# Three elementwise steps of an attention and expert layer put on ScalarE instead of VectorE

## The chip, the core and the metric

The kernel runs on one core of one Trainium2 chip. The metric is the device time of the whole kernel in microseconds, the median over several executions. Five engines work side by side, each through its own queue in order: TensorE (PE in the profile, PEld for its weight loads), VectorE (DVE), ScalarE (ACT), GpSimd (POOL) and SyncE (SP), which issues the transfers.

## The reference

A layer over 8 rows of 512 tokens with 256 features. Each row is normalised, and goes into an attention and a feed-forward part, whose outputs are added to the input.

The attention has 16 heads of 16 features and three branches: attention to 32 compressed blocks of 16 tokens, attention to the tokens of four chosen blocks, and attention to the last 32 tokens. The blocks are chosen by the compressed logits:

```python
logits_c = jnp.where(c_ok, s_b, NEG)
out_c = jnp.einsum('bhtn,bhnd->bhtd', jax.nn.softmax(logits_c, axis=-1), v_c)
_, top_idx = jax.lax.top_k(logits_c, r_eff)            # r_eff = 4
tok = (top_idx[..., None] * G + jnp.arange(G)).reshape(B, H, T, r_eff * G)
```

Three gates from a softmax weigh the branches. The feed-forward part is a gated network with 1024 hidden units, plus a retrieval of experts: for each of 4 heads the top 8 of 64 keys on two axes are taken, the best 8 of the 64 sums of pairs are kept, and each kept pair names one of 1024 experts, weighted by a softmax:

```python
sc, ix = jax.lax.top_k(sim, KPH)                       # KPH = 8
all_ix = (ixx[..., :, None] * NKEYS + ixy[..., None, :]).reshape(b, t, H, KPH * KPH)
scores, pk = jax.lax.top_k(all_sc, KPH)
```

## The kernel before

The work is cut into 8 rows, 32 tiles of 128 tokens (four to a row) and 16 halves of 256 tokens. Each stage is a Python generator that is run over all rows, tiles or halves. Weights stay in SBUF, but for the gated network's first weights, which are loaded again for each half (`fetch`).

**What sets the order.** No order is written by hand. The class `Conductor` (lines 164 to 251) plans: each stage yields the engine and the buffers or events it needs next; the planner takes, among the stages that could start within 0.12 us of the earliest, the one with the lowest rank (the numbers of the `each` lines, 1184 to 1202), lets it issue until its next yield, and books the instructions. Its costs are a fixed part and a part for each element (lines 169 to 171, and a hop from engine to engine). Lines 204 to 210 book that GpSimd and VectorE exclude each other, on VectorE's side only for `tensor_tensor` and `scalar_tensor_tensor` without an operand in PSUM. So the queue of each engine is a result of these costs, and any edit of a stage can change the order of all queues. All instructions go through one helper, so they all have line 160 in the profile's compiled copy; they are told apart by the tiles they write and read.

**The stages that matter here.**
- `layernorm` (479): per row, mean and variance of four tiles (bn_stats, bn_aggr), the square root on ACT, a reciprocal with one correction step, then for each tile `xn` = (x - mean) x rs on DVE (507), two transposes on PE, and a copy to `xnT` by ACT. There is one `xn` buffer.
- `queries` (670): projections and the compressed logits `lg`, with a low value where a block is not allowed.
- `logits` (701): q times k of all tokens up to the tile's end into PSUM; DVE takes block maxima `bm` and window maxima `ml`.
- `select` (758): per head the eight largest compressed logits; the first four are replaced by BIG in a copy `mr` (match_replace, 779); line 783 turns the copy into marks, 0 for a chosen block and -1e30 otherwise; the marks are added to `bm`, the maximum `ms` is taken, and GpSimd writes marks minus `ms` into the extended query `ext`, which PE transposes. `mr` has one buffer.
- `weights` (862) and `products` (913): PE multiplies the extended queries with the keys into pairs of PSUM banks, ACT writes the exponential `wT`, PE multiplies it with the values. There are two pairs, and a step takes both.
- `choose_experts` (977): per tile and head, max and index of the top 8 (`top`, `ixu`), two subtractions into `ed`, the cast of the indices to bf16 `ix` (997), two comparisons with a table (`at_y`, which lies in a `big` buffer, and `at_x`), sums of pairs, their top 8, counts, and the exponentials `et` and `ed` on ACT.
- `route` (1054): four times per tile a comparison into `big` on DVE and several 128x1024 products and sums (`big`, `gw`) on GpSimd.
- `experts`, `hidden`, `project` (1083, 1123, 1165): the large products; ACT and DVE finish `aT`, `xg` and `hT`.

Of the kernel before, what the change touches and what calls it, by code (L numbers as in the profile page):

```python
# [11 lines left out]
AF = mybir.ActivationFunctionType  # L12
ALU = mybir.AluOpType
# [3 lines left out]
P = 128  # L17
# [5 lines left out]
NT = T // P  # L23
# [11 lines left out]
OUT = -1.0e30  # L35
BIG = 3.0e38
HALF_BIG = 1.0e38

_CONST_COLS = [
    ("ident", P), ("any", 1), ("grp", 4), ("head4", H),  # L40
# [59 lines left out]
def bc(ap, axis, n):  # L100
    a = ap.unsqueeze(axis)
    shape = list(a.shape)
    shape[axis] = n
    return a.to_broadcast(shape)
# [150 lines left out]
def tile_kernel(ctx, tc, x, wq, wk, wqT, wv, wo, wck, wcv, wga, bga, wgu, bg, bu, wd, bd,  # L255
# [5 lines left out]
    pe, vec, act, pool, sp = (Engine(con, e, n) for e, n in (  # L261
        (nc.tensor, "PE"), (nc.vector, "DVE"), (nc.scalar, "ACT"), (nc.gpsimd, "POOL"),
        (nc.sync, "SP")))
# [4 lines left out]
    def buf(name, shape, dt=F32):  # L268
        return cp.tile(shape, dt, name=name, tag=name)

    def stock(name, n, shape, dt=F32):
        return Stock(con, [buf(f"{name}{i}", shape, dt) for i in range(n)])
# [18 lines left out]
    def load_x(b, t):  # L291
        sp.dma_start(out=t, in_=x[b].rearrange("(i p) d -> p i d", p=P))
# [55 lines left out]
    bd_s = weight("bd_s", bd.partition_broadcast(P), [P, DM])  # L348
    eps_s = buf("eps_s", [P, 1])
    vec.memset(eps_s, EPS)  # L350
    bgh = buf("bgh", [P, 8])
    vec.tensor_scalar(bgh, bg_s, 0.5, None, ALU.mult)

# [30 lines left out]
    xn1 = stock("xn", 1, [P, DM])  # L384
# [7 lines left out]
    mrs = stock("mr", 1, [P, H, 4 + NB])  # L392
# [8 lines left out]
    top, ixu = buf("top", [P, 2 * PH, KPH]), buf("ixu", [P, 2 * PH, KPH], U32)  # L401
    ix = buf("ix", [P, KPH, 2 * PH], BF16)
# [35 lines left out]
    PE, DVE, ACT, POOL, SP = "PE", "DVE", "ACT", "POOL", "SP"  # L438
# [28 lines left out]
    def to_heads(src, dst):  # L467

        def to_pe(pt):
            for g in range(4):  # L470
                pe.transpose(heads4(pt.ap)[:, g, :], src[:, g].rearrange("p j n -> p (j n)"), ident)
        def to_sb(pt):
            act.copy(dst, heads4(pt.ap))
            pt.free()
        return to_pe, to_sb
# [3 lines left out]
    def layernorm(s):  # L479

        if s.b == 0:
            xl = first_x
            yield DVE,
        else:
            xl = yield SP, xls
            load_x(s.b, xl.ap)
            yield DVE,
        mv, st = buf_mv, buf_st
        for i in range(NT):
            vec.bn_stats(out=st, in_=xl.ap[:, i, :])  # L490
            vec.bn_aggr(out=mv[:, i, :], in_=st)
            yield DVE,
        vec.tensor_scalar(buf_ve, mv[:, :, 1], EPS, None, ALU.add)
        yield ACT,
        act.activation(buf_rs, mv[:, :, 1], AF.Sqrt, bias=eps_s)
        yield DVE,
        rs, cor = buf_rs, buf_cor
        vec.reciprocal(rs, rs)

        vec.tensor_tensor(cor, rs, rs, ALU.mult)  # L500
        vec.tensor_tensor(cor, cor, buf_ve, ALU.mult)
        vec.tensor_scalar(cor, cor, -0.5, 1.5, ALU.mult, ALU.add)
        vec.tensor_tensor(rs, rs, cor, ALU.mult)
        s.xnT = yield None, xnTs
        for i in range(NT):
            xn = yield DVE, xn1
            vec.tensor_scalar(xn.ap, xl.ap[:, i, :], mv[:, i, 0:1], rs[:, i:i + 1],
                              ALU.subtract, ALU.mult)
            pt = yield PE, banks
            p2 = pt.ap[:, :DM].rearrange("p (c n) -> p c n", c=2)  # L510
            for c in range(2):
                pe.transpose(p2[:, c, :], xn.ap[:, c * P:(c + 1) * P], ident)
            xn.free()
            yield ACT,
            act.copy(s.xnT.ap[:, :, i * P:(i + 1) * P], p2)
            pt.free()
        xl.free()
        s.done("xn")

    buf_mv, buf_st = buf("mv", [P, NT, 2]), buf("st", [P, 6])  # L520
    buf_ve, buf_rs, buf_cor = buf("ve", [P, NT]), buf("rs", [P, NT]), buf("cor", [P, NT])

    def prepare_keys(s):
# [234 lines left out]
    def select(t):  # L758

        s, i = t.row, t.i  # L760
        nb = (i + 1) * (P // G)
        yield None, t.ev("lg")
        lg = t.lg.ap
        mr, t.ec = yield None, mrs, ecs
        for h in range(H):
            if h % 4 == 0:
                yield DVE,
            vec.max(out=t8[:, h, :], in_=lg[:, h, 4:4 + nb])
        yield POOL,
        pool.tensor_copy(mx, t8[:, :, 0])  # L770
        pool.tensor_tensor(t.ec.ap, lg[:, :, 4:], bc(mx, 2, NB), ALU.subtract)
        t.done("ec")
        yield DVE,

        vec.memset(t8[:, :, R:], BIG)
        for h in range(H):
            if h % 4 == 0:
                yield DVE,
            vec.match_replace(out=mr.ap[:, h, :4 + nb], in_to_replace=t8[:, h, :],
                              in_values=lg[:, h, :4 + nb], imm_value=BIG)  # L780
        t.lg.free()
        sel = mr.ap[:, :, 4:]
        vec.tensor_scalar(sel[:, :, :nb], sel[:, :, :nb], HALF_BIG, OUT, ALU.is_lt, ALU.mult)
        yield DVE, t.ev("s")
        bmf = t.bm.ap.rearrange("p g j n -> p (g j) n")
        vec.tensor_tensor(bmf[:, :, :nb], bmf[:, :, :nb], sel[:, :, :nb], ALU.add)
        vec.tensor_reduce(ms, bmf[:, :, :nb], AX.X, ALU.max)
        t.bm.free()
        t.qx = {}
        for v in ((2, 0) if i < 2 else (2, 0, 1)):  # L790
            e, t.qx[v] = yield POOL, exts, qxs
            ef = e.ap.rearrange("p g j n -> p (g j) n")
            pool.tensor_copy(ef[:, :, :D], t.q.ap.rearrange("p g j n -> p (g j) n")[:, :, :D])
            if v == 2:
                pool.tensor_scalar(ef[:, :, G:], bc(t.ml.ap.rearrange("p g j -> p (g j)"), 2, G),
                                   -1.0, None, ALU.mult)
                t.ml.free()
            else:
                w = min(G, nb - G * v)
                pool.tensor_tensor(ef[:, :, G:G + w], sel[:, :, v * G:v * G + w], bc(ms, 2, w),  # L800
                                   ALU.subtract)
            pt = yield PE, banks
            to_pe, to_sb = to_heads(e.ap, t.qx[v].ap)
            to_pe(pt)
            e.free()
            yield ACT,
            to_sb(pt)
            t.done(("qx", v))
        mr.free()
        t.q.free()  # L810
# [166 lines left out]
    def choose_experts(t):  # L977

        i = t.i
# [14 lines left out]
        vec.tensor_tensor(ed[:, :, :NK], sim[:, PH:, :], bc(top[:, PH:, 0], 2, NK), ALU.subtract)  # L994
        vec.tensor_tensor(ed[:, :, NK:], sim[:, :PH, :NX], bc(top[:, :PH, 0], 2, NX), ALU.subtract)
        pt.free()
        vec.tensor_copy(ix.rearrange("p j h -> p h j"), ixu)

        ayh = yield DVE, bigs
        at_y = ayh.ap.bitcast(BF16).rearrange("p (j y h) -> p j y h", y=NK, j=KPH)  # L1000
# [12 lines left out]
        yield DVE,  # L1013
        vec.tensor_scalar(pick, pick, HALF_BIG, None, ALU.is_gt)
        with nc.allow_low_precision(reason="counts up to 8"):
# [149 lines left out]
    def project(t):  # L1165
# [16 lines left out]
        t.yo.free()  # L1182

    each(rows, lambda s: 4 * s.b - 3.0, layernorm)
    each(rows, lambda s: 4 * s.b - 2.5, prepare_keys)
    each(rows, lambda s: 4 * s.b - 0.5, prepare_values)
    each(rows, lambda s: 99, release_row)
    each(tiles, lambda t: t.n, queries)
    each(tiles, lambda t: t.n + 0.1, logits)
    each(tiles, lambda t: t.n + 0.2, select)  # L1190
    each(tiles, lambda t: t.n + 0.3, compressed)
    each(tiles, lambda t: t.n + 0.3, weights)
    each(tiles, lambda t: t.n + 0.25, products)
    for jp in range(2):
        each(tiles, lambda t: t.n + 0.24, finish(jp))
    each(tiles, lambda t: t.n + 0.15, choose_experts)
    each(tiles, lambda t: t.n + 0.2, route)
    each(tiles, lambda t: t.n + 0.5, experts)
# [53 lines left out]
```

## Time and profile before

| | |
|---|---|
| Median of three runs | 1812.65 us (1808.81 to 1814.56) |
| Profiled execution | 1813.57 us, span 1811.8 us, granted clock 0.97 |
| VectorE instructions | 5292 |
| ScalarE instructions | 1370, among them 15 table loads (19.2 us) |
| GpSimd: 128x1024 products and sums, big | 224, 486.1 us, mean 2170 ns |
| GpSimd: 128x1024 products and sums, gw | 96, 228.1 us, mean 2376 ns |
| ScalarE: exponentials wT | 224, 217.6 us, mean 1021 ns |

The profile is one execution. "Busy" is the time in which an engine has an instruction running. The groups give a mean duration; the view of one tile gives the smallest, median and largest. The waits name the engine and the tile that a waiting instruction needed last. The chain of work that ended last is followed back from the last instruction, at each step to what released it or to the instruction before it on its engine.

### The profile page before, as it was taken

The numbers are of one execution on the slowest core, as the hardware profiler recorded it, in microseconds if no ns is written. First come the engines' busy times: TensorE is split into PE (matmuls) and PEld (weight loads), VectorE is DVE, ScalarE is ACT, GpSimd is POOL, SyncE is SP. The second block draws the span as 40 slices with busy tenths as digits, with TensorE's granted clock in tenths as the row PEclk, the third lists the DMA queues.
The fourth block names the chain that finished last, engine by engine and source line by source line (L and its number), as shares of the span: only waits on it lengthen the run. The fifth ranks groups of instructions, "written<-read, shape, count | busy, mean of one in ns | idle before, by whom it ended". The sixth has DMA issues, their size and how long they took to land.

```text
span 1811.8 us, 47633 instructions
## 1 busy us (share of the span) xinstructions
PE 1622.0 (90%) x19208; PEld 1246.5 (69%) x19208; DVE 1478.4 (82%) x5292; ACT 686.5 (38%) x1370; POOL 1012.4 (56%) x789
## 2 busy tenths in 40 slices
PE   3889879899899998999989998989979999898969
PEld 2667757777677766767667676766757777676757
DVE  2598799886977889898898967788897897979892
ACT  1344323444335243352343533344324434433233
POOL 2066546646475365665476754656647456575644
PEclk9999989999999999999999998999989999998989
DMA  5001001111001100001011110101001010100001
GB/s 181 10 21 37 19 19 31 31 40 24 24 25 37 37 26 25 24 26 38 16 34 31 32 31 20 36 26 37 25 18 31 15 40 28 31 19 24 25 11 32
DMA packets 55069, 56.12 MB, mean 31 GB/s; under 512 B 21696, under 2 KB 38080, under 8 KB 54848
## 3 DMA queue, kind: packets, MB, share of 16 engines
q1 hardware_dynamic: 54848, 53.07, 9.8%
q8 instruction: 151, 2.47, 0.6%
q14 instruction: 70, 0.57, 0.1%
HBM read 48.02 MB, written 4.19 MB: 29 GB/s over the span
## 4 chain that ended last, share of the span: by engine, by line
PE 55%; DVE 36%; ACT 3%; issue 3%; POOL 1%; DMA 1%; SPq 0%; DVEq 0%; ACTq 0%; POOLq 0%
PE psum L160 55%; DVE bm L160 6%; DVE big L160 4%; DVE pick L160 3%; DVE ixu L160 2%; DVE ml L160 2%; DVE mr L160 2%; DVE aT L160 2%; ACT wT L160 2%; DVE junk L160 2%; DVE hT L160 1%; DVE sums L160 1%; DVE top L160 1%; DVE at_x L160 1%; DVE xg L160 1%
## 5 line engine op out<-in xcount | busy, mean ns | idle before, releaser
L160 POOL TENSOR_TENSOR big<-big,ed 128x1024 f32<-128x1024 f32 x224 | 486.1, 2170 | 411.9 <-DVE big L160 359.2
L160 ACT ACTIVATE wT<-psum 128x1024 f32<-128x1024 f32 x224 | 217.6, 1021 | 167.6 <-PE psum L160 167.6
L160 PE MATMUL psum<-xnT,wb 128*128 128x256 f32 x1024 | 255.2, 393 | 9.1 <-DVE hT L160 5.6
L160 POOL TENSOR_TENSOR gw<-gw,big 128x1024 f32<-128x1024 f32 x96 | 228.1, 2376 | 7.0
L160 DVE TENSOR_REDUCE bm<-psum 128x32 f32<-128x512 f32 (+2 forms) x224 | 199.1, 911 | 32.3 <-PE psum L160 32.1
L160 PEld LDWEIGHTS psum<-xnT,wb 128*128 128x128 f32 x1024 | 191.7, 196 | 46.7 <-DVE hT L160 8.2
L160 DVE SCALAR_TENSOR_TENSOR big<-rc 128x1024 f32<-128x1024 f32 x128 | 167.6, 1309 | 19.5 <-POOL gw L160 19.5
L160 PE MATMUL psum<-wT,v 128*32 128x128 f32 x3584 | 138.4, 279 | 25.7 <-ACT wT L160 24.9
L160 PE MATMUL psum<-qx,k 32*128 32x128 f32 (+1 forms) x4352 | 149.6, 271 | 11.0 <-DVE ml L160 9.1
L160 PEld LDWEIGHTS psum<-qx,k 32*128 32x128 f32 (+1 forms) x4352 | 123.8, 175 | 38.9 <-issue 17.8
L160 PEld LDWEIGHTS psum<-wT,v 128*32 128x32 f32 x3584 | 86.6, 109 | 78.7 <-ACT wT L160 50.6
L160 PE MATMUL psum<-xnT,deT_s 128*128 128x128 f32 x1024 | 131.9, 284 | 5.0 <-DVE aT L160 2.7
L160 PEld LDWEIGHTS psum<-xnT,deT_s 128*128 128x128 f32 x1024 | 126.0, 199 | 12.1 <-DVE aT L160 3.7
L160 PE MATMUL psum<-wd_s,hT 128*128 128x256 f32 x512 | 121.1, 382 | 0.0
L160 DVE SCALAR_TENSOR_TENSOR aT<-aT,psum 128x512 f32<-128x512 f32 x128 | 87.3, 682 | 38.9 <-ACT aT L160 31.4
L160 PE MATMUL psum<-k,q 32*128 32x384 f32 (+3 forms) x1024 | 113.9, 486 | 5.2 <-DVE ml L160 3.7
L160 PE MATMUL psum<-ue_s,aT 128*128 128x256 f32 x512 | 117.1, 381 | 0.0
L160 ACT ACTIVATE xg<-psum,bgh 128x256 f32<-128x256 f32 x128 | 60.7, 474 | 142.3 <-PE psum L160 140.1
L160 PEld LDWEIGHTS <-cbf 128*128 128x128 bf16 x856 | 69.1, 102 | 58.7 <-issue 30.6
L160 PEld LDWEIGHTS psum<-ue_s,aT 128*128 128x128 f32 x512 | 95.2, 190 | 15.5 <-issue 2.0
L160 PEld LDWEIGHTS psum<-wd_s,hT 128*128 128x128 f32 x512 | 94.1, 190 | 15.1 <-issue 2.6
L160 ACT COPY qx<-psum 128x512 f32<-128x512 f32 x80 | 47.0, 587 | 140.1 <-PE psum L160 126.9
(161 smaller groups left out, 3170.5 us busy)
## 6 DMA issues: line engine op xcount, KB each, us to landing
wb<-in_wgu SPq DMA_DIRECT2D x128, 256.0 KB, 2.6
xl<-in_x SPq DMA_DIRECT2D x8, 512.0 KB, 3.9
yo<-in_x SPq DMA_DIRECT2D x32, 128.0 KB, 2.1
out<-yo SPq DMA_DIRECT2D x32, 128.0 KB, 1.7
vl<-v SPq DMA_DIRECT2D x96, 8.5 KB, 1.8
deT_s<-in_deT SPq DMA_DIRECT2D x1, 1024.0 KB, 5.2
wd_s<-in_wd SPq DMA_DIRECT2D x1, 1024.0 KB, 7.6
ue_s<-in_ue SPq DMA_DIRECT2D x1, 1024.0 KB, 10.0
```

The source lines that it names most:

```text
L160: return f(*a, **k)
```

## The change

Three steps go from VectorE to ScalarE:

- the normalization: `xn` = Identity(x x rs + (-mean x rs)); the new column `mrs` = -mean x rs is made once per row by one small VectorE instruction
- the marks: match_replace now writes MARK = 2^110 in place of the chosen logits, and ScalarE adds -2^110 to all. A chosen logit becomes exactly 0; any other, being far smaller, vanishes in the rounding and becomes about -2^110
- the cast of the top 8 indices to bf16

```diff
+MARK = 2.0 ** 110
...
+    big_s = buf("big_s", [P, 1])
+    vec.memset(big_s, -MARK)
...
         s.xnT = yield None, xnTs
+        vec.scalar_tensor_tensor(buf_mr, mv[:, :, 0], -1.0, rs, ALU.mult, ALU.mult)
         for i in range(NT):
-            xn = yield DVE, xn1
-            vec.tensor_scalar(xn.ap, xl.ap[:, i, :], mv[:, i, 0:1], rs[:, i:i + 1],
-                              ALU.subtract, ALU.mult)
+            xn = yield ACT, xn1
+            act.activation(xn.ap, xl.ap[:, i, :], AF.Identity, scale=rs[:, i:i + 1],
+                           bias=buf_mr[:, i:i + 1])
...
+    buf_mr = buf("mrs", [P, NT])
...
             vec.match_replace(out=mr.ap[:, h, :4 + nb], in_to_replace=t8[:, h, :],
-                              in_values=lg[:, h, :4 + nb], imm_value=BIG)
+                              in_values=lg[:, h, :4 + nb], imm_value=MARK)
         t.lg.free()
         sel = mr.ap[:, :, 4:]
-        vec.tensor_scalar(sel[:, :, :nb], sel[:, :, :nb], HALF_BIG, OUT, ALU.is_lt, ALU.mult)
+
+        yield ACT,
+        act.activation(sel[:, :, :nb], sel[:, :, :nb], AF.Identity, bias=big_s)
         yield DVE, t.ev("s")
...
         pt.free()
-        vec.tensor_copy(ix.rearrange("p j h -> p h j"), ixu)
+        yield ACT,
+        act.copy(ix.rearrange("p j h -> p h j"), ixu)
```

The numbers of instructions on PE, GpSimd and SyncE stay; VectorE's program has 87 fewer and ScalarE's 96 more.

## Prediction

> **What bounds the kernel now.** I read first the busy shares and the chain of work that ended last, then what TensorE (PE) waits for, then the instructions that the change moves, and last the busy time of each engine in the stretches where those instructions stand on the chain.
>
> ```profile
> PE 1622.0 (90%) x19208; PEld 1246.5 (69%) x19208; DVE 1478.4 (82%) x5292; ACT 686.5 (38%) x1370; POOL 1012.4 (56%) x789
> PE 55%; DVE 36%; ACT 3%; issue 3%; POOL 1%; DMA 1%; SPq 0%; DVEq 0%; ACTq 0%; POOLq 0%
> ```
>
> Two engines carry the end together: PE and VectorE (DVE). ScalarE (ACT) is idle 62% of the span and hardly on the chain. No one engine is the bound. The queues run in a fixed order, so the span is PE's 1622 us plus what PE waits (190 us). What PE waits for, largest rows:
>
> ```profile
> PE psum L160 <- DVE atc L160: 31.1, 10, 8.3
> PE psum L160 <- ACT wT L160: 24.9, 41, 3.6
> PE psum L160 <- DVE aT L160: 17.9, 15, 2.8
> PE psum L160 <- DVE at L160: 13.3, 13, 2.8
> PE psum L160 <- DVE ml L160: 12.8, 18, 1.8
> PE psum L160 <- DVE xn L160: 10.8, 6, 6.2
> ```
>
> The columns are total us, times and the longest. All rows of that view with DVE as releaser sum to 106 us, those with ACT to 50, POOL 8, DMA 16. So at most some 106 us lie open to a lighter DVE, and 50 us can grow if ACT gets later.
>
> **The change, part by part.** The three moved groups, with min/median/max ns of one:
>
> ```profile
> L160 DVE TENSOR_SCALAR xn<-xl,mv,rs x32: 399/466/2161, 28.0 to 1415.9; 128x256 f32<-128x256 f32 x32
> L160 DVE CAST ix<-ixu x32: 298/664/2227, 73.4 to 1724.6; 128x64 bf16<-128x64 uint32 x32
> L160 DVE TENSOR_SCALAR mr<-mr x32: 226/394/2043, 87.1 to 1757.0; 128x128 f32<-128x128 f32 x8, 128x256 f32<-128x256 f32 x8, 128x384 f32<-128x384 f32 x8, 128x512 f32<-128x512 f32 x8
> ```
>
> The maxima near 2.1 us have one cause: in the timeline the cast at 1512.52 runs 2.15 us while GpSimd's gw add runs from 1512.15 to 1514.50, and ends just after it. I read it so: these DVE forms stand still while such a GpSimd instruction runs. The planner books such exclusion for tensor_tensor and scalar_tensor_tensor alone, so these waits are not in its order.
>
> Removed from DVE: busy 29.9 (xn) + 29.3 (ix) + 21.8 (mr; 2.1 + 4.4 + 7.3 + 8.0) = 81.0 us. Not all of it goes. In the timeline the cast is followed at once by at_y (big<-cbf,ix) in 15 of 32 cases, and the mark by the bm add in 15 of 32; both can stand still in the same way, so there the wait only moves one instruction on. Above the minima, ix holds 29.3 - 32 x 0.298 = 19.8 us and mr 21.8 - 8 x (0.226 + 0.293 + 0.360 + 0.427) = 11.4 us; 15/32 of both is 14.6 us. The eight new [128,4] products (-mean x rs) cost 8 x 0.16 (row rs<-rs,cor) = 1.3 us, 6 at most (row cor<-cor, mean 767 ns). The memset of big_s is one 59 ns instruction ahead of a 21.9 us wait for bg_s, which hides it; without that cover it costs those 59 ns. DVE loses about 81.0 - 14.6 - 1.3 = 65 us, to 78%.
>
> Added to ACT: xn at 474 ns (row xg<-psum,bgh, same size and a bias tile) x 32 = 15.2; ix between 223 (rc<-psum 128x64) and 259 (et), 241 x 32 = 7.7; marks at about 300, 474, 555, 636 ns (rows wp, xg, between, ec) x 8 = 15.7. Sum 38.6 us, ACT 725 us or 40%. Identity already runs in hidden(), and the built order has 15 table loads in both kernels, so no table load is added.
>
> Here a rule speaks against the change. The Trainium skill, "ScalarE: Activation LUTs", section "Rules for kernel authors", sends adds and multiplies to VectorE, since it does more elements in the same time. By undisturbed minima that holds here: 12.8 + 9.5 + 10.4 = 32.7 us of DVE against 38.6 us of ACT, a loss of 6 us of engine time. By the means it doesn't: 81.0 against 38.6. The rule prices DVE alone; GpSimd, busy 56%, makes the difference. I sum with the means.
>
> What of this lies on the path: cut into short windows, the chain holds xn in 15 pieces (14.4 us), ix in 13 (13.1) and the marks in 13 (7.5; told from match_replace by their start times), 35 us. Of the waits that only move on, the same share (35/81 x 14.6 = 6 us) comes back: **29 us off the path** if the chain is taken at its word. It may not be. Busy time of PE and DVE in five of the largest pieces:
>
> ```profile
> 311.58:313.39 1.81, 1.81 (x19) 1.81 (x18) 1.80 (x2) 0.58 (x1) 1.73 (x2) 1.00 0.20 72
> 1019.87:1022.00 2.13, 2.13 (x88) 1.76 (x80) 2.13 (x5) 0.43 (x2) 2.05 (x2) 1.00 0.44 131
> 1203.16:1204.87 1.71, 1.47 (x9) 0.90 (x6) 1.71 (x5) 0.74 (x2) 1.63 (x2) 1.00 0.06 5
> 1512.60:1514.67 2.07, 2.07 (x51) 1.58 (x50) 2.07 (x5) 1.34 (x5) 1.90 (x1) 1.00 0.00 0
> 1667.24:1669.39 2.15, 2.15 (x71) 1.34 (x69) 2.14 (x1) 1.15 (x3) 2.07 (x2) 1.00 0.28 27
> ```
>
> After each window's length come PE, PEld, DVE, ACT, POOL. PE was busy in nearly all of it, with work it had in hand; the delay is paid later (after 1669.55 the chain shows 2.65 us without cause). The lower end is 106/647 (PE's waits for DVE over DVE's time on the chain) of 29 us = 5. The skill's "Perfetto Trace Analysis", section "Identifying the Most-Contended Engine", calls matmul busy time a poor measure of how full TensorE is and prefers weight-load time, here 69%: by it these stretches have room and the 29 us stand. I take 29, since a late DVE delays every later meeting of the two queues.
>
> New waits of DVE for ACT: at_y now waits for ix and the bm add for the marks, 64 answers. Nearest row: DVE aT <- ACT aT, 31.4 us over 64 = 0.49 us each, 31 us at most; at least 0. In the built order 63 of the 64 have other DVE work between, often big<-rc (1.3 us) or aT (0.68), against 0.24 to 0.64 us on ACT. I take a quarter, 8 us of DVE, of which DVE's 36% of the chain is **3 us on**.
>
> New waits of ACT for DVE: ix waits for the index search, the mark for the last match_replace, and all evictions queued behind stand too. Nearest row:
>
> ```profile
> ACT et L160 <- DVE et L160: 99.5, 27, 9.5
> ```
>
> That is 3.1 us for each of 32, behind a DVE sequence of 7.1 us (at_y to et by mean durations), so 0.44 per us. Ahead of ix stand 4.9 us, ahead of the marks 4.1: 2.15 and 1.8 us each, 126 us of standing ACT in all. How much reaches PE? The chain runs through et's exponential 4 times of 32, 12.5%: **16 us on**. Ends: 0, and all of what PE waits for ACT against what ACT waits for DVE (50 of 125 us, 40%): 50 us. For xn the operands are ready long before; PE's 10.8 us for xn stay, now released by ACT, and I put the edit there at nothing beyond the engine time: ACT's idle 62% hides it, and without that cover all 15.2 us would count.
>
> Queues: PE, GpSimd and SyncE issue the same instructions as before, and no DMA is moved by the edits themselves. But the planner orders every queue from its costs, and in the built kernel under half of DVE's and about a third of ACT's instructions keep their sequence. Its price is unsigned. The stores of each row's last tile leave 205.6, 212.6, 221.3, 209.4, 225.6, 208.5 and 201.4 us apart for the same work: 8 us of scatter from order and phase, in part made good by the next row; I take 15 us for the whole as its error.
>
> Sum: 1813.57 (profiled execution) - 29 + 3 + 16 = 1803.6. The median shown is 0.9 lower, so 1803 us.
>
> **Rivals.**
> *PE hides it* (chance 0.15). The windows above speak for it: PE 9.6 of 9.9 us busy. Relief is then 5 us, and the ACT terms shrink with it to about 3: 1811 us. Against it: PE waits 106 us for DVE somewhere.
>
> *ACT stands in front of PE's evictions* (0.35), the slower side. In the built order the next instruction on ACT after ix is an exponential wT in 17 of 32 cases; behind ed before, it was 6 of 32. PE's next logits need the PSUM pairs that wT frees, and PE already waits for wT 41 times. If those 17 waits pass in full, 17 x 2.15 = 37 us, and an eighth of the other 89 us, 11: 1812.65 - 29 + 3 + 48 = 1835; half passed gives about 1822, and I'd say 1830. It decides as soon as more than (29 - 3)/126 = 21% of ACT's standing time reaches PE. Against it: a lighter DVE is less late, and one wait on DVE shortens the next.
>
> *Relief wins* (0.50), 1803, its own range 1780 to 1807.
>
> **How the numbers follow.** About 0.3% (5.4 us) is what a measurement of this kernel can tell from no change. Of relief's 0.50, 0.45 is faster and 0.05 the same; the hidden case splits into 0.03 faster, 0.10 the same, 0.02 slower; of the ACT case's 0.35, 0.33 is slower and 0.02 the same: faster 0.48, same 0.17, slower 0.35. The range takes relief with a kind order below (1803 - 29) and the ACT case with some of its scatter above: 1774 to 1838.
>
> **What would show it.** Right: DVE busy near 1413 us and PE's waits for DVE under 90 us; at_y and the bm add with higher means (1475 and about 620 ns now); xn near 474 ns on ACT. Wrong toward slower: ACT ix and ACT mr waiting over 126 us for DVE together, PE's row for ACT wT well over 25 us. Wrong in the relief: PE's waits for DVE unchanged though DVE is lighter. If the time moves over 15 us with these waits unchanged, the new order did it, not the moved instructions.

## The result and the profile after

The changed kernel takes 1801.1 us (median of 8 runs, 1792.96 to 1805.67) against 1812.9 us of the kernel before beside it. The ratio is 0.9928, 95% interval 0.9909 to 0.9947: 0.7% faster. The forecast was 1803 us, faster. The profiled execution took 1801.37 us, with a span of 1799.6 us, 12.2 us less than before.

The busy shares and the chain of the changed kernel:

```profile
PE 1615.6 (90%) x19208; PEld 1248.7 (69%) x19208; DVE 1459.7 (81%) x5205; ACT 730.2 (41%) x1466; POOL 1017.0 (57%) x789
PE 57%; DVE 35%; issue 3%; ACT 3%; SPq 1%; DMA 1%; DVEq 0%; ACTq 0%
```

VectorE lost 18.7 us of busy time. That is the surprise of this page: instructions of 81.0 us left it, and 65 us of relief were forecast. ScalarE gained 43.7 us. Where the difference went is seen in the instructions that stayed, here two that read what the moved ones write, before (L160) and after (L161; smallest, median and largest duration in ns):

```profile
L160 DVE TENSOR_TENSOR at_x<-cbf,ix x32: 411/419/2594, 74.9 to 1726.2; 128x512 bf16<-128x512 bf16 x32
L160 DVE TENSOR_TENSOR bm<-bm,mr x32: 284/548/2594, 88.3 to 1757.4; 128x128 f32<-128x128 f32 x8, 128x256 f32<-128x256 f32 x8, 128x384 f32<-128x384 f32 x8, 128x512 f32<-128x512 f32 x8
L161 DVE TENSOR_TENSOR at_x<-cbf,ix x32: 409/422/2587, 79.5 to 1720.2; 128x512 bf16<-128x512 bf16 x32
L161 DVE TENSOR_TENSOR bm<-bm,mr x32: 284/554/2536, 85.8 to 1749.7; 128x128 f32<-128x128 f32 x8, 128x256 f32<-128x256 f32 x8, 128x384 f32<-128x384 f32 x8, 128x512 f32<-128x512 f32 x8
```

Their smallest and median durations are those of before, but more of them last over 2 us: of the 32 at_x 2 did before and 9 do now, of the 32 bm adds 2 and now 5. In all at_x took 24.4 us before and takes 37.2 us now, the bm add 19.7 and now 25.7 us. The queue of PE waits as follows (total us, times, longest), the rows that answer to those shown before:

```profile
PE psum L161 <- DVE aT L161: 23.1, 18, 4.8
PE psum L161 <- ACT wT L161: 19.5, 37, 1.2
PE psum L161 <- DVE hT L161: 18.3, 17, 3.6
PE psum L161 <- DVE ml L161: 16.1, 17, 1.8
PE psum L161 <- DVE atc L161: 15.8, 7, 6.1
PE psum L161 <- DVE at L161: 12.4, 9, 5.5
...
PE psum L161 <- ACT xn L161: 9.4, 4, 6.5
```

All rows with VectorE as releaser sum to 101.9 us (105.9 before), those with ScalarE to 59.0 (53.7). The wait for xn (10.8 before, 9.4 now) only changed its column, from VectorE to ScalarE. Without xn the waits for VectorE rose from 95.1 to 101.9 us, those for ScalarE fell from 53.7 to 49.6, and those for GpSimd, 8.0 before, are gone. All of PE's waiting, span less busy time, fell by 5.8 us (189.8 to 184.0), and PE's own busy time by 6.4. So the kernel is faster by about what was forecast, while PE waits no less for VectorE. For unchanged waits and a move of over 15 us the prediction had named the order, not the moved instructions, as the cause; the move is 12 us, so its own sign leaves the matter open. That had to be tested.

### The profile page after: what moved, and what is told of

Same layout as the page of the kernel before. It is cut to its first block, busy times and chain, and to the rows that moved or that the text cites. A ratio compares the mean times of both kernels' runs of the same rounds, so it can differ in the third digit from the quotient of the medians.

```text
span 1799.6 us, 47624 instructions
## 1 busy us (share of the span) xinstructions
PE 1615.6 (90%) x19208; PEld 1248.7 (69%) x19208; DVE 1459.7 (81%) x5205; ACT 730.2 (41%) x1466; POOL 1017.0 (57%) x789
## 4 chain that ended last, share of the span: by engine, by line
PE 57%; DVE 35%; issue 3%; ACT 3%; SPq 1%; DMA 1%; DVEq 0%; ACTq 0%
PE psum L161 57%; DVE bm L161 5%; DVE big L161 5%; DVE pick L161 2%; DVE ixu L161 2%; DVE ml L161 2%; DVE aT L161 2%; DVE at_x L161 2%; DVE sums L161 1%; DVE junk L161 1%; DVE top L161 1%; DVE mr L161 1%; DVE hT L161 1%; ACT wT L161 1%; DVE xg L161 1%
## 5 line engine op out<-in xcount | busy, mean ns | idle before, releaser
L161 POOL TENSOR_TENSOR big<-big,ed 128x1024 f32<-128x1024 f32 x224 | 490.0, 2188 | 406.9 <-DVE big L161 345.8
L161 ACT ACTIVATE wT<-psum 128x1024 f32<-128x1024 f32 x224 | 218.7, 1024 | 145.0 <-PE psum L161 144.9
L161 PE MATMUL psum<-xnT,wb 128*128 128x256 f32 x1024 | 259.0, 398 | 19.1 <-DVE hT L161 7.1
L161 POOL TENSOR_TENSOR gw<-gw,big 128x1024 f32<-128x1024 f32 x96 | 234.6, 2444 | 6.9
L161 PEld LDWEIGHTS psum<-xnT,wb 128*128 128x128 f32 x1024 | 194.7, 198 | 55.8 <-DVE hT L161 8.9
L161 DVE TENSOR_REDUCE bm<-psum 128x32 f32<-128x512 f32 (+2 forms) x224 | 199.2, 911 | 36.3 <-PE psum L161 36.2
L161 DVE SCALAR_TENSOR_TENSOR big<-rc 128x1024 f32<-128x1024 f32 x128 | 169.1, 1321 | 15.3 <-POOL gw L161 13.7
L161 PE MATMUL psum<-qx,k 32*128 32x128 f32 (+1 forms) x4352 | 151.0, 270 | 14.1 <-DVE ml L161 10.5
L161 PEld LDWEIGHTS psum<-qx,k 32*128 32x128 f32 (+1 forms) x4352 | 124.3, 174 | 44.7 <-issue 18.8
L161 PE MATMUL psum<-wT,v 128*32 128x128 f32 x3584 | 136.0, 278 | 19.4 <-ACT wT L161 18.8
L161 PE MATMUL psum<-xnT,deT_s 128*128 128x128 f32 x1024 | 131.9, 284 | 13.4 <-DVE aT L161 10.8
L161 PEld LDWEIGHTS psum<-xnT,deT_s 128*128 128x128 f32 x1024 | 124.5, 198 | 20.7 <-DVE aT L161 14.3
L161 PEld LDWEIGHTS psum<-wT,v 128*32 128x32 f32 x3584 | 87.1, 109 | 68.5 <-ACT wT L161 39.1
L161 PE MATMUL psum<-wd_s,hT 128*128 128x256 f32 x512 | 123.7, 387 | 0.4 <-DVE hT L161 0.4
L161 PE MATMUL psum<-ue_s,aT 128*128 128x256 f32 x512 | 117.2, 381 | 0.0
L161 DVE SCALAR_TENSOR_TENSOR aT<-aT,psum 128x512 f32<-128x512 f32 x128 | 87.1, 680 | 35.1 <-ACT aT L161 24.2
L161 PE MATMUL psum<-k,q 32*128 32x384 f32 (+3 forms) x1024 | 109.7, 481 | 5.7 <-DVE ml L161 5.6
L161 ACT ACTIVATE xg<-psum,bgh 128x256 f32<-128x256 f32 x128 | 60.7, 474 | 133.2 <-PE psum L161 129.0
L161 PEld LDWEIGHTS <-cbf 128*128 128x128 bf16 x856 | 69.0, 101 | 60.9 <-issue 30.6
L161 PEld LDWEIGHTS psum<-ue_s,aT 128*128 128x128 f32 x512 | 95.1, 190 | 15.9 <-issue 3.2
L161 PEld LDWEIGHTS psum<-wd_s,hT 128*128 128x128 f32 x512 | 94.3, 192 | 16.8 <-issue 3.3
L161 PE MATMUL psum<-cbf 128*128 128x512 bf16 (+2 forms) x344 | 93.6, 374 | 7.7 <-DVE bm L161 7.4
```

What stands on the lines that cost most here:

```text
L161: return f(*a, **k)
```

## Experiments

Two theories. *Relief*: VectorE does less, stands still less for GpSimd, and PE waits less for it. *Order*: the planner, fed with other costs, made other queues, and those happened to be better. Ratios are to the kernel before, measured beside each run. A profile is one execution, and PE's busy time scatters: e1 and e11 are the same kernel, and their profiles show 1614.6 and 1621.1 us. So differences of that size in PE's busy time are not read from one profile alone.

| Run | Ratio | 95% interval | Median us |
|---|---|---|---|
| e1: three steps on ScalarE, before's order | 0.9908 | 0.9886 to 0.9930 | 1799.3 |
| e2: three steps on VectorE, the new order | 1.0135 | 1.0108 to 1.0162 | 1840.7 |
| e3: kernel before, choice window 0.11 us | 0.9880 | 0.9857 to 0.9903 | 1794.1 |
| e4: changed kernel, choice window 0.11 us | 0.9904 | 0.9880 to 0.9928 | 1797.7 |
| e5: normalization alone, before's order | 0.9944 | 0.9930 to 0.9958 | 1805.6 |
| e6: cast alone, before's order | 0.9953 | 0.9934 to 0.9972 | 1808.1 |
| e7: marks alone, before's order | 1.0016 | 1.0000 to 1.0032 | 1818.1 |
| e8: three steps on ScalarE, order of e3 | 0.9804 | 0.9790 to 0.9819 | 1783.2 |
| e9: as e8, marks left on VectorE | 0.9809 | 0.9790 to 0.9829 | 1781.9 |
| e10: kernel before, most GpSimd products left out | 0.9669 | 0.9654 to 0.9684 | 1756.2 |
| e11: e1 again | 0.9884 | 0.9869 to 0.9900 | 1796.9 |
| e12: e1, most GpSimd products left out | 0.9714 | 0.9699 to 0.9730 | 1764.8 |

**The moved instructions without the new order, e1.** The planner books a VectorE instruction, while a ScalarE one is issued at its place. The other queues keep before's order instruction by instruction.

```diff
-        vec.tensor_copy(ix.rearrange("p j h -> p h j"), ixu)
+        con.book("DVE", "tensor_copy", (ix.rearrange("p j h -> p h j"), ixu), {})
+        nc.scalar.copy(ix.rearrange("p j h -> p h j"), ixu)
```

The other two steps are edited in the same way.

> The three steps run on ScalarE, but the planner still books them as before, so every queue keeps before's order and the moved instructions alone change. Theory relief (taking them off VectorE is what gained): most of the 12 us, 1800 to 1806 us. Rival order (the new plan is what gained): 1810 to 1818 us, or later, since VectorE now waits for ScalarE where the old plan put nothing between. In both, VectorE's busy time falls by no more than about 19 us, as it did after the change, because the standing still moves to the next instructions.

The ratio is 0.9908: all of the gain, with the old order. The last sentence of the expectation was wrong. Busy shares of e1, its waits of PE, and of VectorE for ScalarE:

```profile
PE 1614.6 (90%) x19208; PEld 1243.1 (69%) x19208; DVE 1413.0 (79%) x5205; ACT 729.2 (41%) x1466; POOL 1017.6 (57%) x789
```

```profile
PE psum L161 <- DVE atc L161: 29.0, 8, 8.3
PE psum L161 <- ACT wT L161: 24.3, 44, 1.5
PE psum L161 <- DVE aT L161: 18.1, 16, 2.5
PE psum L161 <- DVE ml L161: 12.6, 17, 1.8
...
PE psum L161 <- ACT xn L512: 9.5, 4, 6.6
```

```profile
DVE bm L161 <- ACT mr L790: 9.7, 16, 0.8
DVE big L161 <- ACT ix L1005: 4.5, 12, 1.3
```

In an unchanged order VectorE loses 65.4 us of busy time, to 1413.0 us: the forecast's own number, though not by the forecast's sum (see below). So the standing still does not have to move on; the new order brought it back. PE's waits for VectorE sum to 83.9 us (before 105.9) and those for ScalarE to 65.3 (53.7). Of both differences some 10 us are only a change of column: PE waits for xn as before (10.8, now 9.5 us), and ScalarE is now its releaser. Without xn, waits for VectorE fall by 11.2 us and waits for ScalarE grow by 2.1; in the second profile of this kernel, e11, the two are 12.7 and 2.5 us. The last view is the price of a hop that the planner did not know of: 14.2 us of VectorE. In the changed kernel, where the planner puts other work between, the two rows are 1.2 and 0.4 us.

**The new order without the moved instructions, e2.** The reverse: booked as in the changed kernel, issued on VectorE as before.

```diff
-        act.copy(ix.rearrange("p j h -> p h j"), ixu)
+        con.book("ACT", "copy", (ix.rearrange("p j h -> p h j"), ixu), {})
+        nc.vector.tensor_copy(ix.rearrange("p j h -> p h j"), ixu)
```

> The planner books the three steps as in the changed kernel, so every queue has the new order, but they run on VectorE as before. Theory relief: no gain, 1811 us or later, since the new order has no place for them on VectorE. Rival order: about 1801 us, all of the gain.

Slower by 1.35%, on the side of relief; the other theory's 1801 us failed. The page of e2:

```profile
PE 1638.3 (89%) x19208; PEld 1262.9 (69%) x19208; DVE 1513.1 (82%) x5293; ACT 687.5 (37%) x1370; POOL 1011.8 (55%) x789
```

The same instructions as before (and the one memset) keep VectorE busy for 1513.1 us in this order, 34.7 us more than in the old one. PE's waits for VectorE are 137.1 us, 120.4 without xn. Against e2, the changed kernel has 53.4 us less on VectorE, and without xn 18.5 us less of those waits; waits for ScalarE are 7.6 us longer. The times give 0.9928/1.0135 = 0.980. So in either order the moved instructions are worth something: 0.9% in the old, 2.0% in the new. Of those 2.0%, 39 us of span, PE's waiting in all is 16.6 us (200.6 to 184.0) and PE's busy time 22.7 us: the five runs of e2 had a granted TensorE clock of 0.955 to 0.961, before 0.968 to 0.973 and the changed kernel 0.967 to 0.974. The last section comes back to the clock.

**What an order alone is worth, e3 and e4.** The planner's window in which it may prefer rank to start time is set from 0.12 to 0.11 us, in the kernel before and in the changed one.

```diff
-    NEAR = 0.12
+    NEAR = 0.11
```

> The kernel before with the planner's choice window at 0.11 us in place of 0.12: the same instructions in another order. It measures what an order alone is worth. Theory relief: within 5 us of 1812.9. Rival order: orders scatter by 10 us and more, so over 8 us away in one direction or the other.

> The changed kernel with the planner's choice window at 0.11 us: the same instructions in another order. Theory relief: the gain stays, 1796 to 1806 us. Rival order: the gain is that of one lucky plan, so 1808 us or later is as likely as 1801.

The kernel before gets 1.2% faster by another order alone, more than the change brought; its VectorE is as busy as ever (1472.2 us). This miss goes against the relief theory's first form: an order is worth 1% and more, so no single re-planned kernel shows what an instruction costs. The changed kernel stays at 0.990 in its other order. Compared at the same window, though, the replanned edit gains nothing at 0.11 us (0.9904 against 0.9880, intervals that overlap) where it gained 0.7% at 0.12 us. That the edit paid when it was replanned is thus in part the luck of one setting of the planner.

**Part by part, e5 to e7**, each booked as in e1, all in before's order.

> Only the normalization runs on ScalarE, in before's order. All three together were 0.92% faster there, some 16.6 us. Theory relief by share of the chain (xn held 14.4 of the 35 us): 7 us faster, ratio about 0.996. Rival (PE waits for xn on either engine, so its latency counts and the relief of VectorE doesn't): 0.999 to 1.003.

> Only the cast of the indices runs on ScalarE, in before's order, where at_y follows it at once in 15 of 32 tiles. Theory relief by share of the chain (13.1 of 35): 6 us faster, ratio about 0.9965. Rival (VectorE's new wait for ScalarE takes the place of the cast): 1.000 or above, and VectorE's wait for ScalarE ix above 10 us.

> Only the marks run on ScalarE, in before's order, where the bm add follows at once in 15 of 32 tiles. Theory relief by share of the chain (7.5 of 35): 3.6 us faster, ratio about 0.998. Rival (the new wait takes the place of the mark): 1.000 or above, with VectorE's wait for ScalarE mr above 10 us.

Normalization and cast each gain half a per cent, the marks nothing. VectorE's busy time falls by 24.7, 19.0 and 21.6 us, together 65.3: the parts add up to e1 (65.4), and the ratios do too (-0.56, -0.47 and +0.16%, together -0.87 against -0.92). The marks relieve VectorE as much as the others. The page of e7, and what ScalarE and VectorE newly wait for in it:

```profile
PE 1628.1 (90%) x19208; PEld 1250.5 (69%) x19208; DVE 1456.8 (80%) x5261; ACT 701.9 (39%) x1402; POOL 1011.4 (56%) x789
```

```profile
ACT mr L787 <- DVE mr L161: 60.4, 27, 11.6
```

```profile
DVE bm L161 <- ACT mr L787: 9.7, 16, 0.8
```

ScalarE stands 60.4 us for match_replace, VectorE 9.7 us for the answer (the rival's row, just under its 10 us). Yet PE's wait in all fell, 189.8 to 185.2 us (span less busy). What ate the gain seems to be PE's busy time, 6.1 us more in this profile, with a clock of 0.961 to 0.966 in eleven of e7's twelve runs. The twelfth had 0.972, as before has beside it, and took 1811.8 us, the fastest of the twelve. Why this kernel is granted less was not tested.

**Relief on top of the better order, e8 and e9.** The edit of e1 with the window of e3; e9 leaves the marks on VectorE.

> The three steps run on ScalarE in the order that the kernel before gets with a choice window of 0.11 us, which was 1.2% faster than before. Theory relief, independent of the order: another 0.9%, ratio about 0.979, 1777 us, which beats both kernels. Rival (relief and order win back the same waits): no better than 0.988, 1794 us.

> Normalization and cast on ScalarE, the marks left on VectorE, in the order with the 0.11 us window. Alone in before's order the parts gave 0.9944, 0.9953 and, for the marks, 1.0016. Theory parts add: 0.9804 less 0.0016, about 0.979. Rival (the marks cost nothing where VectorE has less to do, and relieve it): 0.981 to 0.984.

Relief and order add: 0.9880 and another 0.8% give 0.9804. Both versions beat both kernels by over 1%, at about 1782 us. Whether the marks pay cannot be told: the two intervals lie over each other.

**Is it GpSimd? e10 to e12.** In `route`, GpSimd's products and sums are booked but not issued, save one per tile; the weights of the experts are left out of the computation.

```diff
             yield POOL,
-            pool.tensor_tensor(m, m, bc(ed[:, h, :NK], 1, NX), ALU.mult)
+            con.book("POOL", "tensor_tensor", (m, m, bc(ed[:, h, :NK], 1, NX)), {})
...
-                pool.tensor_tensor(m, m, exb, ALU.mult)
+                con.book("POOL", "tensor_tensor", (m, m, exb), {})
                 yield POOL,
-                pool.tensor_tensor(g3, g3, m, ALU.add)
+                con.book("POOL", "tensor_tensor", (g3, g3, m), {})
```

> The kernel before, its order kept, with GpSimd's 128x1024 work in route cut to one product per tile (the weights of the experts are left out, so the output is not the layer's). Theory standing still: without those GpSimd instructions the maxima of cast, normalization and marks fall to the undisturbed 0.3 to 0.45 us, VectorE's busy time falls by more than 100 us, and the kernel gets 2% or more faster. Rival (the long durations have another cause): the maxima near 2 us stay.

> The three steps on ScalarE in before's order with GpSimd's work complete: the first experiment again, as the partner of the run without GpSimd's products in the same call. Expected as it was, ratio 0.991.

> The three steps on ScalarE in before's order, with GpSimd's 128x1024 work in route cut to one product per tile (the weights of the experts are left out). To be compared with the kernel before under the same cut. Theory standing still (the step pays since GpSimd holds VectorE up): without it the move takes only 33 us of VectorE's time and adds 43 us to ScalarE's, and the two kernels are within 0.3% of each other, or this one is slower. Rival (any VectorE time taken off counts alike): still 0.4% or more faster.

In e10, the kernel before with GpSimd busy 17%, the moved groups and the page read:

```profile
L160 DVE TENSOR_SCALAR xn<-xl,mv,rs x32: 395/408/1677, 27.8 to 1370.5; 128x256 f32<-128x256 f32 x32
L160 DVE CAST ix<-ixu x32: 296/300/310, 73.7 to 1668.8; 128x64 bf16<-128x64 uint32 x32
L160 DVE TENSOR_SCALAR mr<-mr x32: 226/359/510, 87.3 to 1698.7; 128x128 f32<-128x128 f32 x8, 128x256 f32<-128x256 f32 x8, 128x384 f32<-128x384 f32 x8, 128x512 f32<-128x512 f32 x8
```

```profile
PE 1598.4 (91%) x19208; PEld 1234.8 (70%) x19208; DVE 1332.3 (76%) x5292; ACT 686.6 (39%) x1370; POOL 303.7 (17%) x469
```

The cast's largest duration falls from 2227 to 310 ns, with nothing changed on VectorE itself. VectorE as a whole does its work in 146 us less. The one normalization of 1677 ns ended 0.15 us after a GpSimd product into gw that was left. The trace of the kernel before says the same one by one: 33 of the 96 moved instructions lasted over 0.9 us, and each of the 33 ended 0.15 to 0.28 us after the end of a GpSimd instruction that was running within 0.1 us of its start.

With little GpSimd work the move is a loss: e12 at 0.9714 against e10 at 0.9669, 0.5% slower, with intervals that do not overlap. Its page:

```profile
PE 1607.6 (91%) x19208; PEld 1240.6 (70%) x19208; DVE 1304.7 (74%) x5205; ACT 727.6 (41%) x1466; POOL 303.1 (17%) x469
```

The move takes 27.6 us off VectorE there and puts 41.0 us on ScalarE; with xn set aside, PE's waits for VectorE fall by 1.0 us only and those for ScalarE rise by 6.6. PE's waiting in all rises by 4.7 us (155.0 to 159.7), where beside a busy GpSimd it fell by 10.1 (e1) and 12.3 us (e11). The rest of the 13.9 us of span is PE's busy time (1598.4 to 1607.6 us), at a granted clock of 0.970 to 0.977 against 0.978 to 0.982 over all runs. e11, the partner with GpSimd's work complete, repeats e1 (0.9884). So the same edit in the same order changes the time by -0.9 to -1.2% where GpSimd is busy 57% and by +0.5% where it is busy 17%. The sign of the waits turns with it; how much of the 0.5% is the clock's is not separated.

## Why the prediction was right, step by step

The number and the cause, relief of a VectorE that GpSimd holds up, were right. The sum behind the number was right in part by luck: its two large terms were both too big and their errors cancel, and the new order, put down as an unsigned error, took back only a part of the gain. Of the four signs that the prediction named for being right, the changed kernel itself shows one in full: at_y and the bm add have higher means (1510 and 802 ns). VectorE at 1459.7 us and PE's waits for it at 101.9 us miss the 1413 and 90, and xn took 608 ns for 474. In before's order (e1) VectorE is at 1413.0 us and the waits at 83.9. It also read two sums too low: PE's rows for ScalarE come to 53.7 us, not 50, and ScalarE's for VectorE to 132, not 125, which leaves the share of 40% as it is.

- *VectorE loses 65 us*: 65.4 us in before's order (e1), 18.7 in the changed kernel. What the forecast left out is that the order sets how often the others stand still: the two orders differ by 34.7 us for the same instructions (e2 against before). And its sum was right by luck. Records of neighbouring VectorE instructions overlap in the trace, and busy time counts an overlap once. In the trace of before, the time in which only the moved instructions were running is 26.3 us (xn), 23.4 (cast) and 20.6 (marks), together 70.2 of their 81.0 us. So 10.8 us could not leave at all, and only 4.8 us, the 1.5 us of mrs among them (1.3 forecast, 5.1 in the changed kernel), passed to others, not the 14.6 us forecast. By parts: the cast passed on about 4 us (23.4 could leave, 19.0 did; 9.3 forecast), the marks none (20.6 could leave, 21.6 did; 5.3 forecast).
- *29 us off the path*: too much. With xn set aside, PE waits 11 us less for VectorE in e1 and 13 in e11, between the ends of 5 and 29. The windows that showed PE busy beside the moved instructions were a better guide than the chain's shares and the 69% of weight loads, by which the prediction kept the 29.
- *16 us back by a standing ScalarE*: too much as well. In e1 ScalarE stands 81 us for index search and match_replace (126 forecast, 77 in the changed kernel), and the wait for et shrinks from 99.5 to 81.7, as the text against the rival had it: a wait on VectorE shortens the next. PE's wait for ScalarE, without xn, grows by 2.1 us. The row for wT, on which the slower rival rested, went from 24.9 to 24.3, and to 19.5 in the changed kernel. That rival failed. Where GpSimd holds VectorE up less (e12), the kernel does get slower and PE's waits for ScalarE rise by 6.6 us, but its row for wT only from 20.7 to 23.9.
- *3 us for VectorE's waits*: 1.6 us of VectorE's time in the changed kernel; the work between covers them, and 14.2 us where the planner didn't know of them.
- *38.6 us on ScalarE*: 43.7 us. The marks took 404 to 722 ns and xn, which reads two columns, 608 (474 forecast); the cast took 480 ns, twice the 241 taken from rows of the same size (smallest, median and largest in ns):

```profile
L161 ACT CAST ix<-ixu x32: 469/478/503, 77.3 to 1717.8; 128x64 bf16<-128x64 uint32 x32
L161 ACT ACTIVATE xn<-xl,mrs,rs x32: 589/602/631, 28.0 to 1401.6; 128x256 f32<-128x256 f32 x32
```

- *The net, 10 us*: PE's wait in all, span less busy, fell by 10.1 us in e1 (189.8 to 179.7) and 12.3 in e11, but through errors that cancel. The prediction took PE's 1622 us of busy time as given. It is not: over the profiles here it runs from 1598 to 1638 us with the clock, a term that the prediction put at nothing. In e1 it is 7.4 us less, in e11 0.9; in the changed kernel it is 6.4 us less, beside 5.8 us less of waiting.
- *The order as an error of 15 us*: the right size (22 us for e3), and the part of the prediction that mattered most. Its test, "a change over 15 us with unchanged waits is the order", could not see what happened: relief of 0.9% or more and a new order that gives a part of it back (0.9928 against 0.9908 and 0.9884), the sum under 15 us. Only fixing the order parted the two.
- *Minima against means*: the rule to keep adds and multiplies on VectorE was right once most of GpSimd's work was gone (e12), and wrong while it was there (e1). The page behind it, "ScalarE: Activation LUTs" of the Trainium skill, section "Rules for kernel authors", gives its factor for bf16 operations with one source; the three steps here read 32-bit elements. The means were the better price; the price that the busy time confirms is the mean less the overlap, 70.2 us.

## What to carry to other kernels

Where a minimum and a mean of the same instruction lie far apart, price it by the mean, find who holds it up, and remove that one in a trial: here the same move changes the time by -0.9% or +0.5% by it. Before adding up durations, see how much of them overlaps with their neighbours. Where a planner orders the queues, compare an edit with the order held fixed (book the old instruction, issue the new one), since here an order alone was worth over 1%, as much as the edit. Then choose the order by trial: edit and order added up to 2%.

## What the runs showed of the hardware that was not expected

The granted TensorE clock differed from kernel to kernel with the same number of TensorE instructions: over all runs 0.955 to 0.961 for e2, 0.968 to 0.973 for before beside it, 0.978 to 0.982 for e10. PE's busy time in the profiles goes with it: 1638.3, 1622.0 and 1598.4 us. It is no fixed property of a kernel: the five runs of e8 have 0.964 to 0.981. And it does not decide alone: e4 has 0.957 to 0.962 and is still 1% faster than before.

The traces show where the clock falls. It is granted in stretches of 3.41 us or multiples of it, at full or half rate. Two stretches of half rate in the trace of before, each with the 3.41 us ahead of it and after it (length, then busy us of PE, PEld, DVE, ACT and POOL, the clock, and the DMA columns):

```profile
480.36:483.77 3.41, 1.65 (x34) 1.25 (x32) 3.36 (x6) 1.14 (x3) 3.11 (x2) 1.00 0.29 77
483.77:487.18 3.41, 3.41 (x13) 2.01 (x11) 3.22 (x20) 1.94 (x2) 3.33 (x2) 0.50 0.02 5
487.18:490.59 3.41, 3.41 (x91) 2.52 (x94) 3.27 (x5) 0.81 (x2) 0.70 (x2) 1.00 0.28 76
698.81:702.22 3.41, 1.63 (x24) 1.01 (x26) 3.38 (x5) 0.38 (x1) 1.57 (x1) 1.00 0.12 47
702.22:705.63 3.41, 3.41 (x30) 2.18 (x23) 3.24 (x11) 1.18 (x2) 3.25 (x3) 0.50 0.02 5
705.63:709.04 3.41, 3.41 (x76) 2.47 (x78) 3.41 (x3) 1.56 (x3) 1.77 (x1) 1.00 0.21 62
```

PE waited for half of the stretch ahead, and is then busy throughout at half rate. This is so nearly everywhere: ahead of 284 of the 300 half-rate stretches in the fourteen profiles PE was busy less than 60% of the 3.41 us, and so it was in only 114 of 6393 other stretches of that length at full rate. So a wait of PE seems to cost twice, once as waiting and once as slower work behind it, which the prediction's sum did not have. The half-rate time adds up to 162 us in e2, 112 in before and 69 in e10. This is read from traces; no run was made to test it, and which waits of a new order fall so closely together is open.

A bf16 cast of 64 uint32 to a strided place takes 480 ns on ScalarE, against 298 undisturbed on VectorE.
